# The first feed-forward pass: two of three copies of the global channels written by ScalarE, and TensorE in the order of the program

## The chip, the core and the metric

The kernel runs on one core of a Trainium2 chip. The time is device microseconds (us) of one execution, and of several executions the median is given. The core has a matrix engine (TensorE, "PE" in the profile; its weight loads are "PEld"), VectorE ("DVE"), ScalarE ("ACT"), GpSimd ("POOL") and SyncE ("SP"). SP and POOL issue the DMA transfers of this kernel: SP the loads, POOL the stores. Each engine works through its own instructions in order and waits on semaphores for the others.

## The reference, cut to what matters

All data are float32. The input x has the shape (4, 64, 256, 256): images b, channels, rows, columns. Two layers follow each other. The part of the first layer that bears on the change:

```python
proj = conv1x1(layernorm(x), in_proj_w)           # 64 channels
local, glob = split(proj, 2)                      # 32 channels each
v = dwconv3x3(conv1x1(glob, qkv_w))[64:96]        # and q, k
out = attention over channels, weights from q, k  # then times v
x = x + conv1x1(concat(out, lgce(local)), out_proj_w)
h = conv1x1(layernorm(x), ffn_in_w)               # 256 channels, then dwconv, gelu, FFT filter
```

Attention weights, the 1x1 convolution of v, its 3x3 depthwise convolution and the output projection are all linear in `glob`. The kernel folds them, once the attention weights are known, into one 3x3 convolution from the 32 global channels to 64 channels for each image (the weights `wc[b]`).

## The kernel before, in words

The program has stages that run one after the other: stage A (projections and sums), the first feed-forward pass `stage_c1`, then `stage_c2` (depthwise convolutions of the hidden channels), `stage_c3` and `stage_d`. The change is in `stage_c1` alone. On the profile's clock `stage_c1` issues its first load at 1720.76 us, and TensorE's first matmul of `stage_c2` (L882) starts at 3420.85 us.

`stage_c1` goes over 64 pairs (pr, s): s is one of 32 strips of 8 image rows, pr one of two pairs of images. A step n of its loop (L856 to L860) has these parts, written as generators that `_steps` advances in turn, one `yield` each per round:

- `load` (L735) of step n+1, all on SP's queue: `pre` and `resp` (local branch, 512 KB each), `xs` (the input, 1024 KB), and for each of the two images a tile `gp` of 128 partitions x 8 rows x 256 columns. The partitions of `gp` are four groups of 32. Groups 1 and 2 (partitions 32 to 95) hold the global and the local channels of the strip's 8 rows (L745, 512 KB). Group 0 holds the global channels one row higher (L747) and group 3 the global channels one row lower (L749, 256 KB each), so that one matmul over 128 partitions sums the three rows of the convolution. Groups 0, 1 and 3 are thus three copies of the same rows, shifted by one row against each other, and each is loaded from the DRAM tensor `projd`.
- `front` of step n: VectorE makes the mask `mk` (L763, L764). For ra = 0 and ra = 1, TensorE fills two PSUM tiles of 512 columns: twelve matmuls from `gp` (three column shifts, two images, two tiles; L775) and two from `mk` (L779); VectorE adds the input and writes `xm` (L785, four instructions per ra). When `xm` is whole, TensorE transposes it (L796, two tiles in each of two halves), ScalarE copies the result to `xmp` (L797), and the layer norm runs on VectorE and ScalarE (L313 to L323; the square is L316 on ScalarE). POOL stores `xmp` (L800).
- `back` of step n-2: TensorE transposes the normalised rows (L810, four tiles), and ScalarE writes them with scale and bias to `xl` (L812, eight instructions).
- `hidden` of step n-3: for four pairs of rows y, four matmuls (L824); of the four PSUM tiles ScalarE copies two (L830) and VectorE two (L828) to `tb`; POOL stores `tb` to `td` (L839, L840, L842).

A float32 matmul of 512 columns stands in the trace as two records, a transpose of 128 columns as one. Matmuls on 64 rows or 64 columns of the array run in pairs beside each other.

All PSUM tiles that concern the stage come from one pool of six buffers (`mm()`, one bank each). `gp` has four buffers (two steps), `pre`, `xs` and `xl` two or three, `tb` five.

The order of the instructions on each engine is not that of the program text. A planner orders them: each instruction has its place in the program as priority, the planner runs the program through its own cost estimates, and when an engine comes free it gives it the ready instruction of the highest priority. `tc.high_priority()` raises the priority of what stands in it. `tc.manual_schedule(engines={PE})` holds TensorE to the order of the text, while the other engines are still ordered by the planner; stage C3 (L1156) and stage D (L1398) have it already, `stage_c1` does not. The planner's order is fixed before the run; on the chip each engine waits in that order.

Of the kernel before, what the change touches and what calls it, by code (L numbers as in the profile page):

```python
# [11 lines left out]
ALU = mybir.AluOpType  # L12
AX = mybir.AxisListType

C, H, W = 64, 256, 256
# [225 lines left out]
def _steps(*gens):  # L241

    live = [g for g in gens if g is not None]
    while live:
        live = [g for g in live if next(g, 0) is None]
# [4 lines left out]
def kernel(ctx: ExitStack, tc: tile.TileContext, x, packs, fd, out, off):  # L250
    nc = tc.nc
    B = x.shape[0]
    V, S, T, G, SY = nc.vector, nc.scalar, nc.tensor, nc.gpsimd, nc.sync
# [5 lines left out]
    def mm():  # L259
        return ps.tile([128, 512], F32, tag="mm", name="mm")  # L260
# [66 lines left out]
    p = sp1.enter_context(tc.tile_pool(name="pst", bufs=2))  # L327
# [386 lines left out]
    def stage_c1():  # L714
        NS = H // 8
        with ExitStack() as cs:
            p = cs.enter_context(tc.tile_pool(name="pc", bufs=2))
# [3 lines left out]
            t = mm()  # L721
# [6 lines left out]
            t = mm()  # L728
            T.matmul(t[:, 0:1], K("opl2"), K("postb"), start=True, stop=True)
            bx = p1.tile([128, 1], F32, name="bx")  # L730
            V.tensor_copy(bx, t[:, 0:1])
            xf = x.rearrange("b c h w -> (b c) h w")
            ld, xns = {}, {}

            def load(pr, s):  # L735
                pre = p.tile([128, 4 * W], F32, name="pre")
                resp = p.tile([128, 4 * W], F32, name="resp", bufs=3)
                SY.dma_start(pre, pred[pr, s].rearrange("h b c n -> (h b c) n"))
                SY.dma_start(resp, resd[pr, s].rearrange("h b c n -> (h b c) n"))
                gps = []  # L740
                for i in (0, 1):

                    gp = p.tile([128, 8, W], F32, tag="gp", name="gp", bufs=4)
                    pg = projd[2 * pr + i]
                    SY.dma_start(gp[32:96], pg[:, 8 * s:8 * s + 8])  # L745
                    lo = 1 if s == 0 else 0
                    SY.dma_start(gp[0:32, lo:8], pg[0:32, 8 * s - 1 + lo:8 * s + 7])  # L747
                    hi = 7 if s == NS - 1 else 8
                    SY.dma_start(gp[96:128, 0:hi], pg[0:32, 8 * s + 1:8 * s + 1 + hi])  # L749
                    if lo:  # L750
                        G.memset(gp[0:32, 0:1, :], 0.0)
                    if hi == 7:
                        G.memset(gp[96:128, 7:8, :], 0.0)
                    gps.append(gp)
                xs = p.tile([128, 8, W], F32, name="xs")
                SY.dma_start(xs, xf[pr * 128:(pr + 1) * 128, 8 * s:8 * s + 8])
                ld[pr, s] = xs, pre, resp, gps

            def front(pr, s):

                xs, pre, resp, gps = ld.pop((pr, s))
                mk = resp
                V.scalar_tensor_tensor(mk, resp, thr[pr], resp, ALU.is_gt, ALU.max)  # L763
                V.tensor_tensor(mk, mk, pre, ALU.mult)  # L764
                yield

                xm = p.tile([128, 16, 2, 8, 8], F32, name="xm", bufs=1)
                for ra in (0, 1):
                    ts = [(r, mm()) for r in (ra, ra + 2)]
                    for r, t in ts:  # L770
                        tv = t.rearrange("p (y w) -> p y w", y=2)
                        for dx in (1, 0, 2):
                            o, i_ = {0: (slice(1, W), slice(0, W - 1)), 1: (slice(0, W), slice(0, W)), 2: (slice(0, W - 1), slice(1, W))}[dx]
                            for i in (0, 1):
                                T.matmul(tv[i * 64:(i + 1) * 64, :, o], wc[2 * pr + i][:, dx, :], gps[i][:, 2 * r:2 * r + 2, i_],  # L775
                                         start=(dx == 1), stop=False, skip_group_check=True)
                    for r, t in ts:
                        hf = r // 2
                        T.matmul(t, pw[hf * 64:(hf + 1) * 64, :], mk[hf * 64:(hf + 1) * 64, (r % 2) * 512:(r % 2) * 512 + 512],  # L779
                                 start=False, stop=True, skip_group_check=True)  # L780
                    yield
                    for r, t in ts:
                        for k in (0, 1):
                            y = 2 * r + k
                            V.scalar_tensor_tensor(xm[:, :, :, y].rearrange("p g a w -> p (g a) w"),  # L785
                                                   t[:, k * W:(k + 1) * W].rearrange("p (g w) -> p g w", w=8), bx,
                                                   xs[:, y, :].rearrange("p (g w) -> p g w", w=8), ALU.add, ALU.add)
                xmp = p.tile([128, 16, 2 * C], F32, name="xmp")
                xn = p.tile([128, 16, 2 * C], F32, name="xn", bufs=3)
                xns[pr, s] = xn  # L790
                for hf in (0, 1):
                    yield
                    for k in (2 * hf, 2 * hf + 1):
                        t = mm()
                        for i in range(4):
                            T.transpose(t[:, i * 128:(i + 1) * 128], xm[:, k * 4 + i].rearrange("p a y w -> p (a y w)"), ident)  # L796
                        S.copy(xmp[:, k * 4:k * 4 + 4].rearrange("p g c -> p (g c)"), t)  # L797
                    rows = slice(hf * 8, hf * 8 + 8)
                    layernorm(p, xmp[:, rows].rearrange("p g (a c) -> p (g a) c", a=2), xn[:, rows].rearrange("p g (a c) -> p (g a) c", a=2), 16, 1)
                G.dma_start(xmd[pr, s], xmp)  # L800

            def back(pr, s):

                xn = xns.pop((pr, s))
                xl = p.tile([128, 4, 8, W // 4], F32, name="xl", bufs=3)
                xls[pr, s] = xl
                for k in range(4):
                    t = mm()
                    for i in range(4):
                        T.transpose(t[:, i * 128:(i + 1) * 128], xn[:, k * 4 + i], ident)  # L810
                    for a in (0, 1):
                        S.activation(xl.rearrange("p f y (k j t) -> p k t j y f", k=4, t=2)[:, k, a],  # L812
                                     t.rearrange("p (j y t f) -> p t j y f", j=8, y=8, t=2)[:, a], AF.Identity, bias=K("ln2b"), scale=K("ln2w"))
                    if k % 2:
                        yield

            def hidden(s, hf):

                for y in range(4):
                    tb = p.tile([128, 8, B, W // 4], F32, name="tb", bufs=5)  # L820
                    for b in range(B):
                        q = slice(b % 2 * 64, b % 2 * 64 + 64)
                        t = mm()
                        T.matmul(t, inT[q, hf * 128:(hf + 1) * 128],  # L824
                                 xls[b // 2, s][q, :, 2 * y:2 * y + 2].rearrange("p f y t -> p f (y t)"), start=True, stop=True)
                        o, i_ = tb[:, :, b, :], t.rearrange("p (f t) -> p f t", f=8)
                        if b % 2:
                            V.tensor_copy(o, i_)  # L828
                        else:
                            S.copy(o, i_)  # L830
                    y0 = 8 * s + 2 * y
                    tf = tb.rearrange("p (f y) b t -> p f (y b t)", f=4)
                    for i in range(NI):
                        r = y0 - R0 * i
                        if 0 <= r < 32:
                            dst = td[hf][:, i, :, r:r + 2].rearrange("g f r e -> g f (r e)")

                            if hf:
                                G.dma_start(dst[:, 2:4], tf[:, 0:2])  # L839
                                G.dma_start(dst[:, 0:2], tf[:, 2:4])  # L840
                            else:
                                G.dma_start(dst, tf)  # L842
                    yield

            def after(*gens):
                for g in gens:
                    if g is not None:
                        yield from g
# [2 lines left out]
            NP = B // 2  # L851
            seq = [(pr, s) for s in range(NS) for pr in range(NP)]
            load(*seq[0])


            for n in range(len(seq) + 3):  # L856
                if n + 1 < len(seq):
                    load(*seq[n + 1])
                _steps(after(back(*seq[n - 2]) if 1 < n < len(seq) + 2 else None, hidden((n - 3) // 2, (n - 3) % 2) if n > 2 else None),
                       front(*seq[n]) if n < len(seq) else None)  # L860

    stage_c1()

# [575 lines left out]
```

## Time and profile before

| | |
|---|---|
| median of 3 executions | 8637.03 us (8633.92 to 8637.6) |
| the profiled execution: its own time | 8643.85 us |
| the profiled execution: span of the core | 8642.1 us |
| TensorE busy | 8062.2 us (93%) |
| VectorE busy | 5829.0 us (67%) |
| ScalarE busy | 4728.1 us (55%) |
| GpSimd busy | 1078.3 us (12%) |
| DMA moved | 1832.49 MB, mean 212 GB/s |
| mean granted TensorE clock | 0.969 |

A share over the whole span mixes five stages. The rows that matter here are those between about 1720 and 3420 us. "Busy" of TensorE is modelled from the records and holds waits inside a run of matmuls, so it is an upper bound of its work. In the lists of waits, each row names who waited, for whom, and then the total in us, the number of times and the longest.

### The profile page before, as it was taken

How to read it: one execution, taken by the hardware profiler on the slowest of the kernel's cores; microseconds unless marked ns; L12 is line 12 of the kernel's file. 1: busy time of each engine (PE TensorE's matmuls, PEld its weight loads, DVE VectorE, ACT ScalarE, POOL GpSimd, SP SyncE). 2: the span in 40 equal slices, each digit the busy share in tenths (PEclk: the TensorE clock that was granted, in tenths of full speed). 3: DMA queues.
4: the chain of work that ended last, by engine and by line, in shares of the span. 5: the costliest groups of instructions: out<-in, count | busy, mean ns of one | idle time of the engine just before them, and what ended most of it. 6: DMA issues, size and time to landing. Idle time of an engine off the chain costs nothing.

```text
span 8642.1 us, 143479 instructions
## 1 busy us (share of the span) xinstructions
PE 8062.2 (93%) x57518; PEld 4185.5 (48%) x57518; DVE 5829.0 (67%) x8506; ACT 4728.1 (55%) x8291; POOL 1078.3 (12%) x1764
## 2 busy tenths in 40 slices
PE   8999999699999998999999999999997999999998
PEld 6777777444444443333333345555553444444443
DVE  7766666377777775222222258888886888888886
ACT  4455555445555554222222257777774777777776
POOL 1111111212222222000000001101110001010011
PEclk9999999799999999999999999999997999999999
DMA  7777777699999998888888866666643233232332
GB/s 164 160 186 186 182 191 180 177 338 385 393 392 391 389 383 344 298 297 296 296 297 297 298 224 190 187 190 193 187 144 77 59 65 73 59 79 59 62 76 39
DMA packets 1258504, 1832.49 MB, mean 212 GB/s; under 512 B 335600, under 2 KB 1040112, under 8 KB 1196656
## 3 DMA queue, kind: packets, MB, share of 16 engines
q1 hardware_dynamic: 1053296, 1034.63, 40.1%
q0 software_dynamic: 204544, 788.69, 28.8%
q8 instruction: 455, 7.45, 0.3%
q14 instruction: 209, 1.71, 0.1%
HBM read 967.65 MB, written 788.53 MB: 203 GB/s over the span
## 4 chain that ended last, share of the span: by engine, by line
PE 60%; ACT 18%; DVE 16%; issue 4%; DMA 2%; SPq 0%; POOL 0%; ACTq 0%; DVEq 0%; POOLq 0%
PE mm L882 12%; PE mm L889 6%; PE mm L775 4%; PE mm L620 4%; PE mm L824 3%; PE mm L1145 3%; PE mm L1367 2%; ACT xl L812 2%; ACT ln_sq L316 2%; PE mm L1384 2%; ACT hg L1369 2%; DVE xn L314 2%; DVE ln_s L1207 2%; PE mm L1043 2%; DVE xc L1209 2%
## 5 line engine op out<-in xcount | busy, mean ns | idle before, releaser
L915 DVE TENSOR_TENSOR y<-ge,mm 128x512 f32<-128x512 f32 (+1 forms) x640 | 406.0, 635 | 1212.8 <-ACT ge L914 1212.8
L882 PE MATMUL mm<-t,w 128*128 128x512 f32 (+1 forms) x2560 | 1094.2, 566 | 18.8 <-DMA t<-td 18.8
L914 ACT ACTIVATE ge<-mm 128x512 f32<-128x512 f32 (+1 forms) x640 | 354.7, 554 | 1253.7 <-PE mm L889 1253.7
L775 PE MATMUL mm<-gp,wc 128*64 128x510 f32 (+1 forms) x3072 | 701.7, 595 | 90.0 <-DVE xm L785 51.8
L620 PEld LDWEIGHTS mm<-wqk,gp 128*128 128x128 f32 x6144 | 728.5, 197 | 98.8 <-issue 60.8
L882 PEld LDWEIGHTS mm<-t,w 128*128 128x128 f32 x2560 | 455.4, 190 | 647.6 <-issue 437.0
L620 PE MATMUL mm<-wqk,gp 128*128 128x128 f32 x6144 | 762.0, 282 | 1.1 <-POOL gp L589 0.9
L1367 PE MATMUL mm<-xfT,w 64*128 64x512 f32 x2048 | 618.1, 640 | 53.8 <-ACT hg L1369 29.8
L1369 ACT ACTIVATE hg<-mm,b 128x512 f32<-128x512 f32 x1024 | 633.9, 688 | 53.4 <-PE mm L1367 51.6
L830 ACT COPY tb<-mm 128x512 f32<-128x512 f32 x512 | 300.8, 588 | 631.7 <-PE mm L824 631.1
L889 PE MATMUL mm<-t,w 64*64 64x504 f32 (+1 forms) x5120 | 575.6, 555 | 0.0
L824 PE MATMUL mm<-xl,pack_c 64*128 64x512 f32 x2048 | 512.1, 601 | 8.0 <-ACT xl L812 4.7
L1384 PE MATMUL mm<-hg,pack_d 128*64 128x512 f32 x2048 | 514.3, 624 | 0.0
L775 PEld LDWEIGHTS mm<-gp,wc 128*64 128x64 f32 x3072 | 277.5, 137 | 468.8 <-issue 331.2
L316 ACT ACTIVATE ln_sq<-xn 128x1024 f32<-128x1024 f32 x256 | 274.7, 1073 | 365.7 <-DVE xn L314 365.6
L318 DVE TENSOR_REDUCE ln_v<-ln_sq 128x16 f32<-128x1024 f32 x256 | 312.0, 1219 | 185.0 <-ACT ln_sq L316 185.0
L1391 POOL DMA_DIRECT2D out_dram<-st x128 | 209.1, 1638 | 1760.0 <-DVE fe L695 1543.6
L1385 DVE TENSOR_SCALAR st<-mm,pack_d 128x512 f32<-128x512 f32 x256 | 280.5, 1096 | 119.6 <-PE mm L1384 119.3
L828 DVE COPY tb<-mm 128x512 f32<-128x512 f32 x512 | 344.2, 683 | 24.1 <-PE mm L824 18.5
L1367 PEld LDWEIGHTS mm<-xfT,w 64*128 64x128 f32 x2048 | 222.7, 191 | 275.8 <-issue 126.1
L1211 ACT ACTIVATE ln_sq<-xc 128x1024 f32<-128x1024 f32 x256 | 272.7, 1066 | 134.2 <-DVE xc L1209 134.2
L889 PEld LDWEIGHTS mm<-t,w 64*64 64x64 f32 x5120 | 158.1, 132 | 374.4 <-issue 374.4
(458 smaller groups left out, 15244.3 us busy)
## 6 DMA issues: line engine op xcount, KB each, us to landing
t<-td SPq DMA_DIRECT2D x256, 1152.0 KB, 10.2
td<-tb POOLq DMA_DIRECT2D x144, 1024.0 KB, 15.6
td<-tb POOLq DMA_DIRECT2D x288, 512.0 KB, 13.9
yd<-y POOLq DMA_DIRECT2D x128, 1152.0 KB, 10.1
ya<-yd SPq DMA_DIRECT2D x192, 512.0 KB, 8.4
xs<-in_x_dram SPq DMA_DIRECT2D x128, 512.0 KB, 6.9
projd<-pj POOLq DMA_DIRECT2D x256, 256.0 KB, 5.8
gp<-projd SPq DMA_DIRECT2D x128, 512.0 KB, 9.4
```

The source lines that it names most:

```text
L316: S.activation(sq, xc, AF.Square)
L620: T.matmul(qp[:, k * 128:(k + 1) * 128], gp[:, 2 * i + k // 2, at + dx:at + dx + 128], wqk[:, dx, :], start=(dx == 0), stop=(dx == 2))
L775: T.matmul(tv[i * 64:(i + 1) * 64, :, o], wc[2 * pr + i][:, dx, :], gps[i][:, 2 * r:2 * r + 2, i_], start=(dx == 1), stop=False, skip_grou ...
L824: T.matmul(t, inT[q, hf * 128:(hf + 1) * 128], xls[b // 2, s][q, :, 2 * y:2 * y + 2].rearrange("p f y t -> p f (y t)"), start=True, stop=True)
L828: V.tensor_copy(o, i_)
L882: T.matmul(t[:, :n], w[:, 0:128], x_[:, c, :], start=True, stop=False, skip_group_check=True)
L889: T.matmul(t[po:po + 64, :n].rearrange("p (n c) -> p n c", c=64)[:, :, o], w[q:q + 64, 128:192], x_[q:q + 64, c, i_], start=False, stop=Tr ...
L914: S.activation(ge[:, :n], ts[0][k][:, :n], AF.Gelu)
L915: V.tensor_tensor(y[:, c, :].rearrange("p n c -> p (n c)"), ge[:, :n], ts[1][k][:, :n], ALU.mult)
L1367: T.matmul(t, w1[rh * 64:(rh + 1) * 64, k * 128:(k + 1) * 128], xT[rh * 64:(rh + 1) * 64], start=True, stop=True)
L1369: S.activation(g, t, AF.Gelu, bias=b1[:, k:k + 1])
L1384: T.matmul(y[rh * 64:(rh + 1) * 64, :], w2[:, k, :], hg[k * 2 + rh], start=False, stop=(k == 1), skip_group_check=True)
```

## The change

The loads of the two shifted groups of `gp` shrink to the one row that the strip itself does not hold (32 KB instead of 256 KB). A new generator `shift` makes the other seven rows of each with ScalarE, from group 1 of the same tile: four copies of 32 partitions x 1792 elements per step. It works for step n+1 while step n runs, and its first copy comes two rounds after the round in which the step begins. The evictions to `xm` (L785) get high priority. `front` has one more `yield` before its transposes, and comes first in a round, ahead of `back` and `hidden`. The loop stands under `manual_schedule` for TensorE.

```diff
                     SY.dma_start(gp[32:96], pg[:, 8 * s:8 * s + 8])
-                    lo = 1 if s == 0 else 0
-                    SY.dma_start(gp[0:32, lo:8], pg[0:32, 8 * s - 1 + lo:8 * s + 7])
-                    hi = 7 if s == NS - 1 else 8
-                    SY.dma_start(gp[96:128, 0:hi], pg[0:32, 8 * s + 1:8 * s + 1 + hi])
-                    if lo:
+                    if s > 0:
+                        SY.dma_start(gp[0:32, 0:1], pg[0:32, 8 * s - 1:8 * s])
+                    else:
                         G.memset(gp[0:32, 0:1, :], 0.0)
-                    if hi == 7:
+                    if s < NS - 1:
+                        SY.dma_start(gp[96:128, 7:8], pg[0:32, 8 * s + 8:8 * s + 9])
+                    else:
                         G.memset(gp[96:128, 7:8, :], 0.0)
...
+            def shift(pr, s):
+
+                gps = ld[pr, s][3]
+                for k in range(2):
+                    yield
+                for gp in gps:
+                    S.copy(gp[0:32, 1:8], gp[32:64, 0:7])
+                    yield
+                    S.copy(gp[96:128, 0:7], gp[32:64, 1:8])
+                    yield
...
-                            V.scalar_tensor_tensor(xm[:, :, :, y].rearrange("p g a w -> p (g a) w"),
...
+                            with tc.high_priority():
+                                V.scalar_tensor_tensor(xm[:, :, :, y].rearrange("p g a w -> p (g a) w"),
...
                 xns[pr, s] = xn
+                yield
                 for hf in (0, 1):
                     yield
...
-            for n in range(len(seq) + 3):
-                if n + 1 < len(seq):
-                    load(*seq[n + 1])
-                _steps(after(back(*seq[n - 2]) if 1 < n < len(seq) + 2 else None, hidden((n - 3) // 2, (n - 3) % 2) if n > 2 else None),
-                       front(*seq[n]) if n < len(seq) else None)
+            _steps(shift(*seq[0]))
+
+
+            with tc.manual_schedule(engines={mybir.EngineType.PE}):
+                for n in range(len(seq) + 3):
+                    if n + 1 < len(seq):
+                        load(*seq[n + 1])
+                    _steps(front(*seq[n]) if n < len(seq) else None,
+                           after(back(*seq[n - 2]) if 1 < n < len(seq) + 2 else None, hidden((n - 3) // 2, (n - 3) % 2) if n > 2 else None),
+                           shift(*seq[n + 1]) if n + 1 < len(seq) else None)
```

More of the change, by code (lines that the diff above doesn't have):

```diff
@@ L784, in front @@
                             y = 2 * r + k
-                            V.scalar_tensor_tensor(xm[:, :, :, y].rearrange("p g a w -> p (g a) w"),
-                                                   t[:, k * W:(k + 1) * W].rearrange("p (g w) -> p g w", w=8), bx,
-                                                   xs[:, y, :].rearrange("p (g w) -> p g w", w=8), ALU.add, ALU.add)
+                            with tc.high_priority():
+                                V.scalar_tensor_tensor(xm[:, :, :, y].rearrange("p g a w -> p (g a) w"),
+                                                       t[:, k * W:(k + 1) * W].rearrange("p (g w) -> p g w", w=8), bx,
+                                                       xs[:, y, :].rearrange("p (g w) -> p g w", w=8), ALU.add, ALU.add)
                 xmp = p.tile([128, 16, 2 * C], F32, name="xmp")
```

## The prediction

> **What bounds the pass now.** I read the busy times by stretch, then TensorE's timeline over one step, then the waits, then the DMA. In the stretches (length, then busy time and records of PE, PEld, DVE, ACT, POOL, then clock, DMA share, GB/s) nothing has much room:
>
> ```profile
> 2150.00:2350.00 200.00, 188.51 (x934) 91.30 (x934) 158.33 (x217) 109.13 (x189) 43.13 (x62) 1.00 1.02 389
> 2350.00:2550.00 200.00, 190.26 (x944) 92.81 (x942) 157.52 (x217) 110.28 (x190) 43.62 (x62) 1.00 1.01 391
> ```
>
> PE is 95% busy, DVE 79%, ACT 55%, and the DMA engines hold packets all the time. TensorE's timeline shows one step:
>
> ```profile
> 2403.13 1.13 PE L779 MATMUL mm<-resp,pw 64*128 64x512 f32 x4
> 2404.09 3.96 PE L824 MATMUL mm<-xl,pack_c 64*128 64x512 f32 x16
> 2407.98 1.09 PE L796 MATMUL mm<-pack_k,xm 128*128 128x128 f32 x8
> 2409.00 1.99 PE L824 MATMUL mm<-xl,pack_c 64*128 64x512 f32 x8
> 2410.92 1.09 PE L796 MATMUL mm<-pack_k,xm 128*128 128x128 f32 x8
> 2411.85 2.19 PE L810 MATMUL mm<-pack_k,xn 128*128 128x128 f32 x16
> 2414.41 5.43 PE L775 MATMUL mm<-gp,wc 128*64 128x512 f32 x24 [0.36 <-ACT xmp L797]
> 2419.76 1.13 PE L779 MATMUL mm<-resp,pw 64*128 64x512 f32 x4
> 2420.72 1.88 PE L824 MATMUL mm<-xl,pack_c 64*128 64x512 f32 x8
> 2423.51 5.36 PE L775 MATMUL mm<-gp,wc 128*64 128x512 f32 x24 [0.90 <-DVE xm L785]
> 2428.80 1.13 PE L779 MATMUL mm<-resp,pw 64*128 64x512 f32 x4
> ```
>
> From L779 to the same L779 a step later (2403.13 to 2428.80) are 25.67 us. By differences of starts the parts are 0.96 + 3.89 + 1.02 + 1.92 + 0.93 + 2.20 + 5.35 + 0.96 + 1.89 + 5.29 = 24.41 us of matmuls, and 0.36 + 0.90 = 1.26 us of visible waits. Up to the last such L779 at 3358.66, 37 steps later, the mean step is 25.82 us; the 0.15 above 25.67 I put down to late loads. The waits (1950 to 3250 us, 51 steps):
>
> ```profile
> ACT tb L830 <- PE mm L824: 509.6, 400, 7.6
> DVE resp L763 <- DMA resp<-resd: 53.5, 34, 3.6
> PE mm L775 <- DVE xm L785: 45.6, 51, 0.9
> PEld mm L775 <- ACT xmp L797: 31.0, 51, 0.9
> PE mm L775 <- DMA gp<-projd: 3.7, 10, 0.4
> ```
>
> ACT waits 10.0 us a step for TensorE: it has room. TensorE waits once a step for the eviction L785, and hardly ever for `gp`. L763 waits for its load, but makes a mask that is used some 45 us later (step 29: L763 at 2425.61, first L779 at 2471.10). So the order on TensorE and the evictions set the step; the DMA stands just below.
>
> ```profile
> DMA packets 111194, 506.14 MB, mean 389 GB/s; under 512 B 13579, under 2 KB 13579, under 8 KB 85352
> gp<-projd SPq DMA_DIRECT2D x128, 512.0 KB, 9.4
> gp<-projd SPq DMA_DIRECT2D x248, 256.0 KB, 10.0
> ```
>
> A step moves pre and resp 1024 KB, gp 2 x (512 + 2 x 256) = 2048, xs 1024, xmd 1024, td (144 x 1024 + 288 x 512)/64 = 4608: 9728 KB = 9.96 MB, 25.6 us at 389 GB/s.
>
> **The change part by part.**
>
> *Loads.* Four transfers of 256 KB become four of 32 KB: 896 KB less a step (9.2%), 8832 KB, 23.2 us at 389 GB/s. Alone this is worth the late loads, 0.15 us a step at most; its use is that the DMA no longer stops a faster step at 25.6. SP still issues nine loads a step in the same order. The small ones cost no more than the row of the large (0.30 to 0.59 us to issue; 32 KB in stage A landed after 7.5 us, the 512 KB here after 9.4).
>
> The Trainium skill ("Perfetto Trace Analysis", Roofline) puts the ceiling of one core's 16 DMA engines at about 435 GB/s, which speaks against this half: by an estimate from it the floor is 22.9 us already before, and fewer bytes buy nothing. The rows here show 389 GB/s with engines always occupied, and never 435.
>
> *Copies.* Four a step on ACT, 32 partitions x 1792 elements, SBUF to SBUF. No such copy is in the trace. The nearest rows:
>
> ```profile
> L316 ACT ACTIVATE ln_sq<-xn 128x1024 f32<-128x1024 f32 x256 | 274.7, 1073 | 365.7 <-DVE xn L314 365.6
> L830 ACT COPY tb<-mm 128x512 f32<-128x512 f32 x512 | 300.8, 588 | 631.7 <-PE mm L824 631.1
> ```
>
> The slope (1073 - 588)/512 = 0.95 ns an element gives 1.80 us, the proportion to L316 gives 1.88; I take 1.85, 7.4 us a step. ACT is busy 110/200 x 25.67 = 14.1 us, so 21.5 after, 88% of a 24.5 us step. Beside other work the copies cost nothing: gp(n+2) is issued when the last L775 of step n ends (2403.20), lands some 10 us later and is needed at 2440, so ACT has over 24 us for them. The cover is gone where a copy stands in front of an eviction: what queues behind it are the PSUM copies L830, L797, L812, and behind those TensorE. Bounds: nothing, and all that ACT has too much in the stretch where it is full. That stretch, four y and two transposes, lasts 3.89 + 1.92 + 1.89 + 1.95 = 9.65 us; ACT needs 8 x 0.59 + 4 x 0.53 = 6.8 in it; with 7.4 more it is 4.6 over. I take 0.24 us, one more of the short waits of the L824 group ("0.24 <-ACT xmp" at 2409.54): landing 10 us after the last L775 puts the copies behind that stretch, beside the next matmuls.
>
> *TensorE in program order, high priority, the new `yield`, `front` first.* One answer for all. The order becomes: two tiles of L810, ra = 0, two of L810, ra = 1, y0, y1, y2, transposes, y3, transposes. Nearly today's, but a y no longer stands between ra = 0 and ra = 1, and the four tiles of `back` come in two pairs. What goes: the 0.90 before L775 (its banks come from L810, freed 5 us earlier; and L785 no longer queues behind a layer norm), the 0.36, and the 0.30 us that L810's last weights wait for `tb` inside its 2.20 ("PEld mm L810 <- DVE tb L828", 15.0 us, 50 times). What comes: eight changes of the array's tile shape instead of seven. Two records take 0.43 us (weight loads at 2423.96, 2424.39, 2424.82), 24 take 5.16, the group takes 5.29: 0.13 a change. POOL issues the same stores; L800 may pass a `td` store, 0.55 us against 0.72 to issue on an engine busy 43 of 200 us: nothing. Next late is the first y after ra = 1, which needs banks of ra = 0 and `back`; ACT has 6 us for them. The bound below: weight loads every 0.43 us mean 6.9 for the 32 L824 records instead of 7.70, so up to 0.8 more could go.
>
> The skill ("TensorEngine Tiling (Array Packing)", Key Properties) says that a change of tiling mode drains TensorE; it names no time, and the 0.13 us above agrees in kind.
>
> *Start.* The four copies for step 0 precede the first L775, +7.4; 896 KB fewer in front of them, -2.3: +5 us once.
>
> **Sum.** 24.41 - 0.30 + 0.13 + 0.24 = 24.48 us a step against 25.82: 1.34 x 60 full steps = 80 us, less 5: 75. From the profiled execution's 8643.85 that is 8569; the median of the runs, 8637.03, lies 6.8 lower, so **8562**.
>
> **Rivals.**
>
> *Floor.* All short waits go: 24.48 - 0.24 - 0.8 = 23.4, next to the DMA's 23.2. 2.4 x 60 - 5 = 139 gained: 8498; at 23.2, 8485. For it: ACT's 10 us of waits. Against: DVE at 20.3 us busy a step and ACT at 21.5 leave little play.
>
> *Nothing changes.* The planner's order is close to the program's already, and the copies' waits eat the 1.3 us: 25.5 to 26, 8625 to 8650. For it: DVE has no spare wait, it stands for ACT at L318 (71.3 us, 102 times) and L313, and a 1.85 us copy ahead of L316 lengthens that.
>
> *Slower: ACT's queue.* The planner puts a ready copy into any gap of ACT, by its own landing times. L763 shows that it does so: 45 us early, and then waiting for the load, 53.5 us over 51 steps. If the copies fall into the y stretch, they stand there for a load that lands late, with L830 behind them. It decides from the fourth copy on: 6.8 + 3 x 1.85 = 12.35 us, just what the stretch (9.65) and six PSUM banks of about 0.45 us each (2.7) carry. The fourth costs 1.9 us a step, without the cushion 4.6: steps of 26.2 to 28.9, 8665 to 8827; I take 27.0, 1.2 x 60 = 71 more: 8713. Against it: the landing above.
>
> **Chances.** Forecast (8525 to 8600) 0.50, floor 0.18, nothing 0.10, slower 0.22. A measurement of this kernel can tell 0.2% (17 us) from no change. Faster 0.67 (the first two, less a little at the edge), same 0.11, slower 0.22. The range runs from the floor, 8485, to 8675, the foot of the slower case, and leaves out most of that case and a little below the floor, under 0.2.
>
> **What would show it.** `gp` loads of 1152 KB a step instead of 2048, 9.04 MB in 24.5 us or some 370 GB/s; four ACT copies of 1.8 to 1.9 us a step; the ra = 1 group starting with no wait for L785; a step of 24.5. Wrong if ACT's waits for `gp` exceed 1 us a step, if PE's weight loads wait for ACT evictions in the y stretch for more than today, or if the copy takes well over 1.9 us.

## The result, and the profile after

The changed kernel takes **8834.69 us** (median of 4 runs, 8827.65 to 8840.32); the kernel before, on the same chip, 8637.32 us. The ratio is **1.0228**, with a 95% interval of 1.0211 to 1.0246: slower. The forecast was 8562.

The mean step, from the first L790 (the old L779, `mm` from `resp`) of step 20 to that of step 60, divided by 40, went from 25.80 to **29.23 us**. (3.43 x 60 full steps = 206 us, and 197 were measured, so the loss lies in the steps.) The line numbers move with the change: L775 is now L786, L779 is L790, L796 is L809, L797 is L810, L810 is L823, L812 is L825, L824 is L837, L828 is L841, L830 is L843; the mask is L774 and L775; the copies are L765 (group 0) and L767 (group 3).

The same stretch as before, in the same columns (length, then busy time and records of PE, PEld, DVE, ACT, POOL, then clock, DMA share, GB/s):

```profile
2350.00:2550.00 200.00, 181.97 (x829) 79.30 (x830) 141.54 (x195) 138.23 (x193) 37.15 (x53) 0.97 0.85 314
```

The DMA fell from a share of 1.01 to 0.85: it no longer bounds the pass. ACT rose from 110 to 138 us, far from full. PE was 95% busy and is 91%. So no engine took over as the bound by its amount of work. TensorE's timeline of one step shows where it stands still (start, length, what, number of records; in brackets the idle time ahead and whom it waited for):

```profile
2427.62 4.82 PE L837 MATMUL mm<-xl,pack_c 64*128 64x512 f32 x20
2433.15 1.13 PE L837 MATMUL mm<-xl,pack_c 64*128 64x512 f32 x4 [0.72 <-ACT tb L843]
2435.47 1.09 PE L809 MATMUL mm<-pack_k,xm 128*128 128x128 f32 x8 [1.19 <-ACT tb L843]
...
2439.84 1.12 PE L837 MATMUL mm<-xl,pack_c 64*128 64x512 f32 x2 [1.19 <-ACT tb L843]
...
2441.82 0.60 PE L823 MATMUL mm<-pack_k,xn 128*128 128x128 f32 x4
...
2443.25 5.36 PE L786 MATMUL mm<-gp,wc 128*64 128x512 f32 x24
...
2450.62 5.36 PE L786 MATMUL mm<-gp,wc 128*64 128x512 f32 x24
```

The four y and two transposes, 9.65 us of matmuls by the forecast's count, last from 2427.62 to 2441.82: 14.20 us. Every bracket in these lines names ScalarE's eviction of PSUM, L843. L786 starts with no bracket, for ra = 0 (2443.25) and for ra = 1 (2450.62): the waits of 0.36 and 0.90 us that stood ahead of these groups are gone. What ScalarE does in such a stretch, one step earlier (the y stretch begins there at about 2398):

```profile
2399.53 0.58 ACT L843 COPY tb<-mm 128x512 f32<-128x512 f32 x1 [3.57 <-PE mm L837]
2400.39 0.58 ACT L843 COPY tb<-mm 128x512 f32<-128x512 f32 x1 [0.27 <-PE mm L837]
2401.68 1.68 ACT L765 COPY gp<-gp 32x1792 f32<-32x1792 f32 x1 [0.71 <-DMA gp<-projd]
2403.28 0.57 ACT L843 COPY tb<-mm 128x512 f32<-128x512 f32 x1
2403.87 1.68 ACT L767 COPY gp<-gp 32x1792 f32<-32x1792 f32 x1
2405.58 0.58 ACT L843 COPY tb<-mm 128x512 f32<-128x512 f32 x1
2406.06 1.68 ACT L765 COPY gp<-gp 32x1792 f32<-32x1792 f32 x1
2407.64 0.57 ACT L843 COPY tb<-mm 128x512 f32<-128x512 f32 x1
2408.24 1.68 ACT L767 COPY gp<-gp 32x1792 f32<-32x1792 f32 x1
```

All four copies stand in the y stretch, one between each two evictions, and the first of them waits for its load. Among the copies an eviction comes every 2.2 us (2403.28, 2405.58, 2407.64); ahead of them, where ScalarE still waits for TensorE, every 0.86 (2399.53 to 2400.39). So TensorE comes to wait for a PSUM bank. The waits of the stage (1950 to 3450 us, some 51 steps) give its size:

```profile
PEld mm L837 <- ACT tb L843: 190.9, 141, 2.2
ACT gp L765 <- DMA gp<-projd: 40.9, 53, 1.5
```

The weight loads L837 wait 3.7 us a step for L843; the corresponding row of before is `PEld mm L824 <- ACT tb L830: 0.2, 1, 0.2` for that whole time. ACT waits 0.8 us a step for `gp`. Of the three signs of being wrong that the prediction names, this is the one about weight loads; the other two did not come (0.8 us of ACT's waits for `gp`, not over 1; a copy of 1.68 us, not over 1.9).

### The profile page after: what moved, and what is told of

It is laid out like the page before. It is cut to its first block, busy times and chain, and to the rows that moved or that the text cites. A ratio compares the mean times of both kernels' runs of the same rounds, so it can differ in the third digit from the quotient of the medians.

```text
span 8838.6 us, 143683 instructions
## 1 busy us (share of the span) xinstructions
PE 8159.0 (92%) x57518; PEld 4156.1 (47%) x57518; DVE 5829.5 (66%) x8506; ACT 5139.2 (58%) x8547; POOL 1075.1 (12%) x1764
## 4 chain that ended last, share of the span: by engine, by line
PE 62%; ACT 18%; DVE 12%; issue 5%; DMA 3%; SPq 0%; POOL 0%; ACTq 0%; POOLq 0%; DVEq 0%
PE mm L898 12%; PE mm L786 7%; PE mm L905 6%; PE mm L620 4%; PE mm L1161 3%; PE mm L1383 3%; DMA gp<-projd 2%; PE mm L1400 2%; ACT hg L1385 2%; PE mm L1059 2%; ACT gp L767 2%; DVE ln_s L1223 2%; PE mm L1030 2%; PE mm L1019 1%; PE mm L986 1%
## 5 line engine op out<-in xcount | busy, mean ns | idle before, releaser
L786 PE MATMUL mm<-gp,wc 128*64 128x510 f32 (+1 forms) x3072 | 690.1, 598 | 17.8 <-ACT gp L767 16.3
L837 PE MATMUL mm<-xl,pack_c 64*128 64x512 f32 x2048 | 593.9, 623 | 97.3 <-ACT tb L843 93.2
L843 ACT COPY tb<-mm 128x512 f32<-128x512 f32 x512 | 294.1, 592 | 248.6 <-PE mm L837 245.7
L837 PEld LDWEIGHTS mm<-xl,pack_c 64*128 64x128 f32 x2048 | 244.0, 191 | 397.8 <-ACT tb L843 221.4
L841 DVE COPY tb<-mm 128x512 f32<-128x512 f32 x512 | 346.0, 686 | 103.7 <-PE mm L837 97.9
L786 PEld LDWEIGHTS mm<-gp,wc 128*64 128x64 f32 x3072 | 210.2, 137 | 408.2 <-issue 374.9
L313 DVE TENSOR_REDUCE ln_s<-xmp 128x16 f32<-128x1024 f32 x128 | 155.2, 1214 | 339.3 <-ACT xmp L810 339.3
```

The costliest lines, as they stand in the source:

```text
L837: T.matmul(t, inT[q, hf * 128:(hf + 1) * 128], xls[b // 2, s][q, :, 2 * y:2 * y + 2].rearrange("p f y t -> p f (y t)"), start=True, stop=True)
```

## The experiments

Theory A, formed from these lines: the cost is the *place* of the copies in ScalarE's queue, between the evictions of the y stretch, where the planner puts them. The rivals were the new order on TensorE, the amount of work added to ScalarE, and later what stands in VectorE's queue. A2 and A3 are later forms of A. Each kernel below is told as an edit of the changed kernel unless another base is named, each time beside runs of the kernel before on the same chip (8634.62 to 8639.77 us). "Step" is always the mean of 40 steps as above.

**e1: the old loads.** The large loads come back, the copies go; order, priority and `yield` stay.

```diff
-                    if s > 0:
-                        SY.dma_start(gp[0:32, 0:1], pg[0:32, 8 * s - 1:8 * s])
+                    SY.dma_start(gp[0:32, lo:8], pg[0:32, 8 * s - 1 + lo:8 * s + 7])
...
-                    S.copy(gp[0:32, 1:8], gp[32:64, 0:7])
-                    S.copy(gp[96:128, 0:7], gp[32:64, 1:8])
```

> The changed kernel with the three loads of gp as before and without the four ScalarE copies; order of TensorE, high priority, the added yield and front first stay. Theory A (the copies stand on ScalarE between the PSUM evictions of the y stretch and cost 29.25 - 25.8 = 3.4 us a step): the step falls to the DMA's 25.6 to 25.8 us, 8620 to 8650 us in all. Rival B (the new order itself costs, the copies only fill waits): the step stays near 29 us, 8790 to 8840 us.

Measured: 8637.35 us, ratio 1.0000 [0.9991, 1.0009], step 25.81. The new order by itself costs nothing and, with the large loads, brings nothing. The whole loss comes with the copies and the small loads.

**e2: TensorE by the planner again.** Only `manual_schedule` goes.

```diff
-            with tc.manual_schedule(engines={mybir.EngineType.PE}):
+            if True:
```

> The changed kernel without manual_schedule: the planner orders TensorE as the other engines; all else stays. The planner gives TensorE in the steady steps the order of the text anyway. Theory A: no difference, 8810 to 8850 us. Rival B (TensorE held to the text waits where the planner would not): under 8700 us.

Measured: 8826.05 us, ratio 1.0219 [1.0204, 1.0234], step 29.13: almost the changed kernel. TensorE's timeline has the same sequence of groups in the steady steps. So the planner makes the new order out of the changed text by itself (`front` first, the new `yield`, the high priority; which of these it needs was not tested), and `manual_schedule` adds nothing to it.

**e3: the copies behind `xl`.** Each pair of copies is held behind the second or the fourth tile of `back` (`issue_after` the last `xl` instruction), a place ahead of the y stretch.

```diff
-                for k in range(2):
-                    yield
                 for gp in gps:
-                    S.copy(gp[0:32, 1:8], gp[32:64, 0:7])
-                    yield
-                    S.copy(gp[96:128, 0:7], gp[32:64, 1:8])
+                    with tc.issue_after(last_xl[0].ins) if last_xl[0] is not None else ExitStack():
+                        S.copy(gp[0:32, 1:8], gp[32:64, 0:7])
+                        S.copy(gp[96:128, 0:7], gp[32:64, 1:8])
                     yield
```

> The changed kernel with the same four copies, but queued on ScalarE behind the xl instructions (L825) of the same step: two behind the second tile, two behind the fourth, so beside the matmuls of L786 and not between the tb copies. Nothing else changes. Theory A: the place of the copies is the cost, not their number or the order of TensorE; the step falls to 24.5 to 25.2 us, 8560 to 8610 us. Rival B: near 29 us, 8790 to 8840 us. Rival C (ScalarE simply has too much work, wherever the copies stand): 27 us or more, over 8710 us.

Measured: 8746.09 us, ratio 1.0126 [1.0109, 1.0142], step 28.13. This met none of the numbers: moving the copies freed only 1.1 us a step. The trace says what came in their stead. First VectorE's timeline, then two rows of the waits (1950 to 3350 us):

```profile
2427.10 1.28 DVE L774 SCALAR_TENSOR_TENSOR resp<-resp,thr 128x1024 f32<-128x1024 f32 x1 [2.67 <-DMA resp<-resd]
```

```profile
DVE resp L774 <- DMA resp<-resd: 206.1, 50, 6.3
PE mm L786 <- DVE tb L841: 129.6, 50, 4.8
```

The mask of a later step stands in VectorE's queue and waits 4.1 us a step for a load that SP issues last, behind the `gp` loads. The eviction L841 is queued behind it, and L786 on TensorE waits for that bank. It is the same fault in another queue: an instruction that is wanted 62.9 us later (mask to first L790 of its step, mean of 40) holds one that is wanted now. In the changed kernel itself L774 waits for only 20.2 us in all; presumably VectorE is late enough there, behind the late matmuls, that the load has landed.

**e4: two copies.** Group 3 is loaded whole again, and only L765 copies (9280 KB a step).

```diff
-                        SY.dma_start(gp[96:128, 7:8], pg[0:32, 8 * s + 8:8 * s + 9])
+                    SY.dma_start(gp[96:128, 0:hi], pg[0:32, 8 * s + 1:8 * s + 1 + hi])
...
-                    S.copy(gp[96:128, 0:7], gp[32:64, 1:8])
-                    yield
```

> The changed kernel with the copy of group 0 alone; group 3 is loaded whole, as before. Two copies a step stand between the tb copies instead of four, and the DMA moves 9280 KB a step. Theory A with a cushion (ScalarE's work in the y stretch fits up to three copies): step 24.5 to 25.2 us, 8560 to 8610 us. Theory A without a cushion (each copy there costs its 1.7 us): 29.25 - 3.4 = 25.8 us, 8640 us. Rival B: near 29 us, 8790 to 8840 us.

Measured: 8750.40 us, ratio 1.0132 [1.0114, 1.0150], step 27.86. Half the copies cost more than was expected of them. One row of the waits (1950 to 3350 us) shows why the run can't settle how the price grows with their number:

```profile
ACT gp L765 <- DMA gp<-projd: 134.5, 55, 6.2
```

With larger loads, the copy waits longer for its tile, some 2.7 us a step (134.5 us over 1400/27.86 = 50 steps), with the evictions behind it. How much of the price of two copies is their length, and how much the waiting, this run doesn't show.

**e5: copies behind `xl`, and the mask late.** e3, and the two mask instructions are held behind the last VectorE copy to `tb` of the y = 2 round of the step before.

```diff
                 mk = resp
-                V.scalar_tensor_tensor(mk, resp, thr[pr], resp, ALU.is_gt, ALU.max)
-                V.tensor_tensor(mk, mk, pre, ALU.mult)
+                with tc.issue_after(last_tb[0].ins) if last_tb[0] is not None else ExitStack():
+                    V.scalar_tensor_tensor(mk, resp, thr[pr], resp, ALU.is_gt, ALU.max)
+                    V.tensor_tensor(mk, mk, pre, ALU.mult)
```

> As e3_behind_xl (copies behind the xl instructions), and the mask of a step (two VectorE instructions that wait for the load of resp) queued behind the third y's last VectorE tb copy of the step before, so one step later than the planner put it; it is then still some 12 us ahead of its use. Theory A2 (with the copies moved, what is left over is VectorE standing for resp, 206 us in 50 steps, with the tb copies behind it): the step falls to 24.5 to 25.5 us, 8560 to 8625 us. Rival C (ScalarE has too much work wherever the copies stand): the step stays at 27 us or more, over 8700 us.

Measured: **8522.08 us** (8521.16 to 8528.67), ratio **0.9870** [0.9856, 0.9885], step 24.06, better than expected and than both kernels. The window, and TensorE from the end of ra = 1 to the next ra = 0 (in this kernel L787, L810, L824 and L838 are the changed kernel's L786, L809, L823 and L837):

```profile
2350.00:2750.00 400.00, 400.00 (x1997) 182.61 (x1996) 336.40 (x464) 345.47 (x466) 88.25 (x126) 1.00 0.98 380
```

```profile
2412.56 5.67 PE L838 MATMUL mm<-xl,pack_c 64*128 64x512 f32 x24
...
2422.03 1.04 PE L824 MATMUL mm<-pack_k,xn 128*128 128x128 f32 x8
2422.99 5.36 PE L787 MATMUL mm<-gp,wc 128*64 128x512 f32 x24
```

TensorE is busy all of the time, as far as the modelled busy time can tell, and no bracket is left. The y stretch lasts 2412.56 to 2422.03 = 9.47 us with the same four copies a step on a ScalarE that is now 86% busy. The 14.20 - 9.47 = 4.73 us, and 0.47 more in the first two tiles of `back` (2441.82 to 2443.25 in the changed kernel, 2422.03 to 2422.99 here), are 5.20 us, all of the 29.23 - 24.06 = 5.17 us between the two kernels: the whole loss lay here. ScalarE's timeline of this step has two copies at 2410.89 and 2412.59, just ahead of the evictions, and the first three evictions of the y stretch close behind them from 2414.30. TensorE waits for none of them; with no further copy among the evictions, the free PSUM banks seem to cover this one delay.

**e13: the mask late, the copies as they were.** The changed kernel with e5's mask alone.

```diff
-                V.scalar_tensor_tensor(mk, resp, thr[pr], resp, ALU.is_gt, ALU.max)
-                V.tensor_tensor(mk, mk, pre, ALU.mult)
+                with tc.issue_after(last_tb[0].ins) if last_tb[0] is not None else ExitStack():
+                    V.scalar_tensor_tensor(mk, resp, thr[pr], resp, ALU.is_gt, ALU.max)
+                    V.tensor_tensor(mk, mk, pre, ALU.mult)
```

> The changed kernel with only the mask moved behind the last VectorE tb copy of the y = 2 round of the step before; the copies stay where the planner puts them. Theory A (the place of the copies is the cost, and the mask matters only once the copies no longer delay it): in the changed kernel VectorE waits for resp only 20.2 us in all, so nothing is taken off the path: a step of 28.5 to 29.3 us, 8790 to 8840 us. Rival (part of the 2.4 us between the changed kernel's step of 29.23 and the 26.82 of the kernel with copies between the tb copies and a late mask is the mask): a step of 27.5 or less, 8730 us or less.

Measured: 8795.18 us, ratio 1.0182 [1.0165, 1.0199], step 28.75. The mask alone gives 0.5 us, the copies' place alone 1.1 (e3), both together 5.2: each hides the other, and neither can be priced by itself.

**e10: the copies back among the evictions, everything else as in e5.** Each copy is held behind the last ScalarE copy to `tb` of the round; the tiles landed long before.

```diff
                 for gp in gps:
-                    with tc.issue_after(last_xl[0].ins) if last_xl[0] is not None else ExitStack():
+                    with tc.issue_after(last_at[0].ins) if last_at[0] is not None else ExitStack():
                         S.copy(gp[0:32, 1:8], gp[32:64, 0:7])
...
-                            S.copy(o, i_)
+                            last_at[0] = S.copy(o, i_)
```

> e5_xl_and_mask with the four copies put back between the tb copies, one behind the second tb copy of each y, but of tiles that landed a step earlier, so that no copy waits for its load. Theory A (a copy in the y stretch costs by its length, ScalarE needs 6.8 + 4 x 1.7 = 13.5 us where TensorE needs 9.6): step 26.2 to 28 us, 8650 to 8765 us. Rival E (the waits for the load behind ScalarE's queue were the cost, the place is harmless once the tile has landed): 24 to 24.6 us, 8515 to 8560 us.

Measured: 8681.96 us, ratio 1.0047 [1.0032, 1.0062], step 26.82. Nothing but the place of the copies differs from e5, in the steps no copy waits for a load, and the step is 2.76 us longer. TensorE, and one row of the waits (1950 to 3350 us; L791, L828 and L842 are the changed kernel's L786, L823 and L837, and L771 is the copy of group 3):

```profile
2420.53 5.87 PE L842 MATMUL mm<-xl,pack_c 64*128 64x512 f32 x24
...
2431.56 1.12 PE L828 MATMUL mm<-pack_k,xn 128*128 128x128 f32 x8
2432.92 6.17 PE L791 MATMUL mm<-gp,wc 128*64 128x512 f32 x24 [0.23 <-DVE tb L846]
```

```profile
PEld mm L791 <- ACT gp L771: 33.0, 53, 0.6
```

The y stretch lasts 2420.53 to 2431.56 = 11.03 us against 9.47 in e5, and the first two tiles of `back` 1.36 against 0.96. The 1.56 us are the price of evictions behind copies that wait for no load: this shows A for the place alone. The 0.40 us hold a wait for VectorE's last eviction of the stretch. The other 0.81 us are of another kind. The copies start at 2423.06, 2425.72, 2428.39 and 2432.00, so the fourth ends after ra = 0 has begun (2432.92). Its matmuls read this tile and wait for the copy itself; they last 6.10 us (to L795 at 2439.02) instead of 5.29. In this kernel two evictions stand between most copies; in the changed kernel and in e13 there is one between each two, and the first copy waits for its load. How much of e13's longer step each of these two makes, the runs don't tell.

**e7: GpSimd makes the copies.** The two lines become `G.tensor_copy`, with the rest as in the changed kernel.

```diff
-                    S.copy(gp[0:32, 1:8], gp[32:64, 0:7])
+                    G.tensor_copy(gp[0:32, 1:8], gp[32:64, 0:7])
```

> The changed kernel with the four copies on GpSimd instead of ScalarE. GpSimd is busy 43 of 200 us and evicts no PSUM. Theory A: if a copy takes up to 4 us, ScalarE's queue is free and the step falls to 24.5 to 26 us, 8560 to 8660 us; the mask's wait for resp may keep it at the upper end. Rival C (copies cost wherever they stand, by contention or by the queue of the stores, which GpSimd issues): 27 us or more, over 8700 us.

Measured: 8726.21 us, ratio 1.0100 [1.0083, 1.0117], step 27.72. The numbers are those of rival C. But the trace has another reason than rival C's: VectorE's wait for `resp` is back, 192.6 us over 51 waits (1950 to 3350 us), as in e3. The next run takes it away.

**e12: GpSimd's copies and the late mask.** e5 with `G.tensor_copy`, not held behind anything.

```diff
-                    with tc.issue_after(last_xl[0].ins) if last_xl[0] is not None else ExitStack():
-                        S.copy(gp[0:32, 1:8], gp[32:64, 0:7])
-                        S.copy(gp[96:128, 0:7], gp[32:64, 1:8])
+                    G.tensor_copy(gp[0:32, 1:8], gp[32:64, 0:7])
+                    G.tensor_copy(gp[96:128, 0:7], gp[32:64, 1:8])
```

> e5_xl_and_mask with the four copies on GpSimd. In e7_gpsimd a copy took 1.67 us alone and 2.2 to 2.6 us beside a VectorE instruction on two SBUF inputs, which itself took 2.7 instead of 1.22 us. Theory: with the mask out of the way GpSimd does as well as ScalarE but for that, 24.1 to 25.2 us a step, 8520 to 8600 us. Rival C: the stores that GpSimd issues come late behind copies that wait for gp, 26 us or more, over 8640 us.

Measured: 8537.79 us, ratio 0.9881 [0.9866, 0.9896], step 24.13. With the mask out of the way, who copies makes 0.07 us a step of difference, so long as no eviction stands behind the copy.

**e9: e5 without the small loads and copies.** The loads of before, no copies, the new order and the late mask.

```diff
+                    SY.dma_start(gp[0:32, lo:8], pg[0:32, 8 * s - 1 + lo:8 * s + 7])
+                    SY.dma_start(gp[96:128, 0:hi], pg[0:32, 8 * s + 1:8 * s + 1 + hi])
...
-                for gp in gps:
-                    with tc.issue_after(last_xl[0].ins) if last_xl[0] is not None else ExitStack():
-                        S.copy(gp[0:32, 1:8], gp[32:64, 0:7])
-                        S.copy(gp[96:128, 0:7], gp[32:64, 1:8])
```

> e5_xl_and_mask with the full loads of gp and no copies: new order and delayed mask alone. Theory A3 (the smaller loads are needed, since 9728 KB a step keep the DMA engines at 25.6 us): step 25.5 to 25.8 us, 8615 to 8640 us. Rival D (the delayed mask and the order are the whole gain of e5): 24.1 to 24.6 us, 8520 to 8560 us.

Measured: 8611.17 us, ratio 0.9965 [0.9951, 0.9979], step 25.20, between the two expectations.

```profile
2350.00:2750.00 400.00, 379.62 (x1858) 171.57 (x1854) 314.03 (x433) 218.20 (x373) 85.60 (x122) 0.97 1.02 398
```

Here the DMA is the bound (share 1.02 at 398 GB/s; 9.96 MB a step in 25.20 us are 395). It shows in bursts: some steps take 24.06 us as in e5, and now and then the evictions wait up to 8.7 us for a store to free their `tb` (`ACT tb L842 <- DMA td<-tb: 64.9, 12, 8.7`, 1950 to 3250 us). Fewer bytes are needed for a step of 24.06; they are worth 25.20 - 24.06 = 1.14 us once nothing else stands in the way. e9 differs from e1 by the late mask alone, so 25.81 - 25.20 = 0.61 us of e1's step was the early mask (its wait for `resp` there: 112.9 us, 50 times, 1950 to 3350 us). This is why the new order alone brought nothing in e1.

**e8: copies in the old order.** The kernel *before*, with the small loads and the four copies as in the change, but without `front` first, the `yield`, the priority and `manual_schedule`.

```diff
+                for gp in gps:
+                    S.copy(gp[0:32, 1:8], gp[32:64, 0:7])
+                    yield
+                    S.copy(gp[96:128, 0:7], gp[32:64, 1:8])
+                    yield
...
                 _steps(after(back(*seq[n - 2]) if 1 < n < len(seq) + 2 else None, hidden((n - 3) // 2, (n - 3) % 2) if n > 2 else None),
-                       front(*seq[n]) if n < len(seq) else None)
+                       front(*seq[n]) if n < len(seq) else None,
+                       shift(*seq[n + 1]) if n + 1 < len(seq) else None)
```

> The kernel before with the small loads and the four ScalarE copies alone: order of TensorE by the planner, no high priority, no added yield, back and hidden first. Theory A: the planner puts the copies between the tb copies here too; step 28 to 29.3 us, 8770 to 8850 us. Rival B (the order is the cost): 25.8 us or less, up to 8645 us.

Measured: 8931.79 us, ratio 1.0345 [1.0329, 1.0360], step 30.80: worse than expected, and 1.57 us a step worse than the changed kernel. With the copies in, the order that was worth nothing in e1 is worth that much.

**e11: e5 in the old order.** e8, with e5's places for copies and mask.

```diff
+                    with tc.issue_after(last_xl[0].ins) if last_xl[0] is not None else ExitStack():
+                        S.copy(gp[0:32, 1:8], gp[32:64, 0:7])
+                        S.copy(gp[96:128, 0:7], gp[32:64, 1:8])
...
+                with tc.issue_after(last_tb[0].ins) if last_tb[0] is not None else ExitStack():
+                    V.scalar_tensor_tensor(mk, resp, thr[pr], resp, ALU.is_gt, ALU.max)
+                    V.tensor_tensor(mk, mk, pre, ALU.mult)
```

> The kernel before with the small loads, the copies behind the xl instructions and the delayed mask, but with the order of before: no manual_schedule, no high priority, no added yield, back and hidden first. Theory A: the 1.26 us of waits of before stay, and back's four tiles stand together, so 25.2 to 25.7 us a step, 8595 to 8630 us: the order half is worth about 1.3 us. Rival D' (the order is worth nothing once copies and mask stand well): 24 to 24.4 us, 8515 to 8545 us.

Measured: 8809.37 us, ratio 1.0194 [1.0178, 1.0209], step 28.77. Both expectations missed. Its waits, 1950 to 3350 us:

```profile
PEld mm L837 <- ACT xl L825: 175.4, 74, 3.7
DVE xm L798 <- PE mm L791: 312.1, 49, 7.6
```

In the old order a y stands between ra = 0 and ra = 1, close behind all four tiles of `back`. It needs banks that those tiles leave only when ScalarE has written `xl`, and ScalarE has two copies among those writes. (By the kernel's text `hidden` reads the `xl` of both pairs of images, and in every second step the later of the two is from step n-2, just written by `back`. There the wait can be for the data as well.) The eviction of ra = 1 comes late in turn. In the new order the whole of ra = 1 lies between the last two tiles of `back` and the first y. So the order and the place belong together: which `xl` writes and evictions are soon wanted decides where a copy does no harm. With the copies and the mask at these places, the order is worth 28.77 - 24.06 = 4.7 us a step.

## Why the prediction was wrong, point by point

- **The step that failed** is the copies' cost: "I take 0.24 us", since "landing 10 us after the last L775 puts the copies behind that stretch". What the runs showed in its place: the planner puts all four copies into the y stretch, the stretch took 14.20 instead of 9.65 us, 4.55 more, and the two tiles of `back` behind it another 0.47. That this meets the term's other end, 4.6 us, so closely is in part luck: the bound was reckoned with copies of 1.85 us and no wait, and the measured 1.68 us would give 6.8 + 4 x 1.68 - 9.65 = 3.9, to which the wait for the load comes. Two things were wrong in the reason for 0.24. The landing of 9.4 to 10 us was a median of the kernel before, with the large loads, and the small loads shorten it. The page after has it:

```profile
gp<-projd SPq DMA_DIRECT2D x128, 512.0 KB, 4.8
```

  In the steps (1950 to 3150 us) it is 5.3 in e5 too, at a DMA share of 0.98, and 7.8 and 10.3 in e9 and e1 with the large loads. And a later landing would not have helped: the copies' place in the queue is fixed before the run, and the first copy did wait for its load there (0.71 us at 2401.68), with L843 behind it. The landing decides how long the queue stands, not where the copy stands. That the planner put it there because its own estimate had the tile ready is argued from the place, not shown.
- **The rival "ACT's queue" was the mechanism**, held at a chance of 0.22, and its value was too mild. It gave 8665 to 8827 us and took 8713; 8834.69 lies 8 us past the end that it named for four copies "without the cushion". The six PSUM banks put the wait off: TensorE runs 20 records of L837 before its first one, but the stretch as a whole still ends the full 4.55 us late. That it "decides from the fourth copy on" was wrong: in e10 three copies stand in the stretch, wait for no load, and lengthen it by 1.56 us. How the price grows from one copy to four, e4 leaves open.
- **The copy's length** was forecast at 1.85 us, within 1.80 to 1.88, and is 1.68 (128 instances of each line, 1679 to 1687 ns). The slope from rows of 128 partitions was a little steep. The Trainium skill ("ScalarE: Activation LUTs", What ACT_TABLE_LOAD costs) gives 186 ns + 0.833 ns an element for an ACTIVATE with immediate scale and bias. The copies stand in the trace as COPY; taken for them too, it is an estimate of 1679 ns for 1792 elements, which the measured 1683 agrees with.
- **The DMA step held.** It gave 25.6 us a step with the old loads and 23.2 with the new: e9 stops at 25.20 with the old, at a little more than the 389 GB/s of the forecast, and e5 runs at 24.06 with the new. That 23.2 can be reached, no run shows. The GB/s of the changed kernel (314, forecast some 370) only follow the longer step.
- **The order's steps held.** The waits of 0.36 and 0.90 us are gone, as the L786 lines at 2443.25 and 2450.62 show. "Next late is the first y after ra = 1 ... ACT has 6 us for them" was right for the first y, which starts without a bracket at 2427.62; the y behind it wait for evictions among the copies, and of those the sentence says nothing. The sum without its copy term is 24.48 - 0.24 = 24.24; e5 measured 24.06, with the mask moved too.
- **The start:** "+5 us once" looks right, and that is luck. The first L779 or L790 is at 1741.4 us before and 1747.3 after, 5.9 later. But the stage's first load is at 1720.8 before and at 1725.2 after, so 4.4 of the 5.9 lie ahead of the stage. From that load to the first L775 or L786 it is 10.9 us before and 11.0 after. To the first L779 or L790 it is 20.6 before, 22.1 after, and in e2, with the same loads and copies, 19.7.
- **A step that was missing:** the mask. The prediction read L763's wait as harmless, because the mask is used 45 us later. It is harmless only while the load lands in time and nothing wanted stands behind it. In e3 it became 4.1 us a step, and no run here has the gain of this change without moving it (e3 and e7 against e5 and e12).

## What to carry to other kernels

When work is added to an engine that evicts PSUM, its length and the engine's idle share say little: ask which instruction will stand directly behind it in the queue, and how soon that one is wanted. A planner that fills gaps by its own estimates may put early work there, as it did with the copies and the mask here, so give such work an explicit place behind an instruction whose result is not soon needed, and do the same for every other early instruction that waits for a load. Where a cost lies between zero and a full bound depending on a position that the schedule fixes, look for how the same schedule placed similar work (here L763) before taking the low end.

## What the runs showed of the hardware that was not expected

- **GpSimd copies float32 as fast as ScalarE**: 32 x 1792 elements in 1.67 us alone (e12, at 2420.86), ScalarE 1.68. But beside VectorE's L323, which reads two inputs from SBUF, both took longer. From e7's timeline of GpSimd and VectorE:

```profile
2406.11 2.21 POOL L765 COPY gp<-gp 32x1792 f32<-32x1792 f32 x1
2406.70 2.70 DVE L323 TENSOR_TENSOR xn<-xn,ln_r 128x1024 f32<-128x1024 f32 x1
```

  The VectorE instruction takes 1.22 us when alone (median of e5). Its end, 2409.40, is close to the copy's end plus 1.22 us, 2408.32 + 1.22 = 2409.54, as if it stood until the copy was done; this is one pair of rows, no test. The Trainium skill ("SBUF — State Buffer", SBUF: two separate sides) names the port that GpSimd and VectorE share as the one point of contention on the engines' side, and these rows agree in kind. Over whole steps it shows as VectorE's busy time, 362.9 of 400 us in e12 against 336.4 in e5, and costs next to nothing there.
- **The DMA's sustained rate** in this pass, at a share of 1.01 to 1.02, is 392 to 398 GB/s (2350 to 2750 us: before 394, e1 392, e9 398).
- **The granted clock** of TensorE in these stretches is 1.00 in e5, which never idles, 0.97 to 0.98 in the changed kernel and 0.94 in e8, which idles most. But before and e9, both with TensorE 95% busy, had 1.00 and 0.97, so it is no plain function of the busy share. Looked at closely, in these kernels the loss comes in short pieces at half clock. In the changed kernel the clock is 0.51 from 2406.60 to 2410.00 us, behind 3.4 us in which TensorE was busy for 1.60; in e9 it is 0.50 from 2376.50 to 2383.30, from the end of a wait of 6.57 us on; the kernel before has no such piece between 1900 and 2800 us (1.00). These pieces cost the changed kernel no time that can be seen: of its steps 20 to 59, the 9 that hold one last 29.23 us on the mean, and the other 31 last 29.23 too.
